# Gate logits of an expert choice taken from another layer's turned tokens, with both scales applied by VectorE

## The chip, the cores and the metric

One Trainium2 chip, one of its cores. The time is the device time of the whole kernel in microseconds (us); lower is better. The kernel before takes 2459.57 us (median of three runs).

## The reference, cut to what matters

Four images x of 56 x 56 tokens with 128 channels pass four layers. The change lies in the last one, on tokens t of shape (4, 3136, 128):

```python
t = t + attn(ln(t))        # scores exp(-|q-k|^2), softmax over them, times V = ln(t) @ Wv.T
t = t + choice(ln(t))

def choice(x):             # 64 experts choose tokens
    logits = einsum('bsd,ed->bse', x, gate_w) + gate_b
    probs = softmax(logits, axis=1)                 # over the tokens
    vals, idx = top_k(probs.transpose(0, 2, 1), 8)  # 8 tokens for each expert
    pooled = einsum('bked,bke->bed', x[idx], vals)
    out = mlp_of_each_expert(pooled)                # weight1, gelu, weight2
    return zeros.at[idx].add(out * vals)
```

ln takes the mean from each token and divides by the deviation. Where all scores of `attn` are far below what float32 tells from 0, its output is the same for each token: the mean of V. The kernel computes that mean, checks by bounds (`bounds`, `decide`) that the scores are so, and has a second program for inputs where they are not.

## The kernel before, in words

An image has NT = 28 tiles of P = 112 tokens, in NG = 7 groups of GT = 4 tiles (GW = 448 tokens). x lives in SBUF with tokens on partitions. A product over channels needs them turned: ScalarE normalises a group to `xn` (`normal`, L1693, four instructions), TensorE transposes it in four (`transposed`, L208) and ScalarE copies the result out of PSUM.

Stages: layer 0 for all images (to about 575 us), then the softmax attention of layer 2 for images 0 to 3 (`Attention.run`; s_ps L2066 the scores, e L2073 the exponentials, o_ps L2149 the products with the values; to about 2246 us), then a tail for image 3 and the experts. While the attention of image i runs, the other layers of earlier images run as *background*: each is a list of pieces with a cost (`costing`), lists are merged by their due places (`merged`), and `Paced` calls pieces between the attention's matmuls. `background(2)` holds the mixture and far attention of images 0 and 1 and the choice of image 0; `background(3)` the same for image 2 and the choice of images 1 and 2; `trail` starts image 3's. The order of each engine is settled when the program is built and does not move at run time. SP (SyncE) issues nearly all DMAs, in its order.

`FarAttention.image` makes, for each group, `xn`, `xnT` (with the sums for the mean), `products` (q_near, k_near) and `with_norms`; `mean` turns the sums into v (L1880 to L1887), and `add` adds v to every token (L1892; image 3: groups 3 and up on GpSimd). `ExpertChoice.steps` then needs, for the tokens x + v:

- `statistics`: L2301, four an image group on VectorE
- `root`: `moments` (L936 to L939), then 1/deviation by Newton steps on VectorE (`inverse_root`, L914 to L924), and the offset L2307
- `store`: x and rs to DRAM `rows`, 129 floats a token, for the gather
- `tokens`, `turned`, `logits`: normalised tokens (L1693, or L1688 on GpSimd), four transposes (L208), copy zT (L2322), matmul with gate_w (L2327), copy to `taken` (L2331), maximum of eight (L2332)
- `choose`: the top eight over the image (L2350), where they are (L2351), the gather of their rows; `marked`, `weighed`, `gather`, `pooled`: exponentials and the mean of the chosen tokens

Image 3's last mixture group, its mean, adds, statistics, roots, logits and choice stand in an order written out by hand (`manual_schedule` in `layers_of_safe_scores`), with `beside` putting bounds between them. There GpSimd makes some roots as a power (`span_norms`, L1673). `experts` then streams the weights of 64 experts, four at a time: 32 lots of 1 MB (L2263), nine ahead. Each step ends with a copy `found` out of PSUM (L2482) and four DMAs to `out0` and `out1` (L2489); `found` has two buffers. `scatter` spreads the outputs to the tokens (L2529, L2541).

PSUM banks of kind "one" (`flow.one`, four) serve all the small products.

Of the kernel before, what the change touches and what calls it, by code (L numbers as in the profile page):

```python
# [9 lines left out]
F32 = mybir.dt.float32  # L10
BF16 = mybir.dt.bfloat16
AF = mybir.ActivationFunctionType
ALU = mybir.AluOpType
# [4 lines left out]
B, H, W, C = 4, 56, 56, 128  # L18
# [1681 lines left out]
class FarAttention:  # L1700
# [13 lines left out]

    def __init__(self, env, ctx, flow, work):
        self.env, self.flow, self.work = env, flow, work
        nc, ins = env.nc, env.ins
        self.cp = cp = ctx.enter_context(env.tc.tile_pool(name="d_const", bufs=1, side="right"))  # L1720
        self.small = ctx.enter_context(env.tc.tile_pool(name="d_small", bufs=2, side="right"))

        self.even = ctx.enter_context(ExitStack())
        self.held = [
            stack.enter_context(env.tc.tile_pool(name=name, bufs=1, side="right"))
            for stack, name in ((ctx, "d_odd"), (self.even, "d_even"))
        ]


        norm = work.tile([128, GW], F32, tag="xnT_m", name="norm")[:, : 2 * 129]  # L1730
        norm = norm.rearrange("p (i c) -> p i c", i=2)
        nc.sync.dma_start(norm, ins["norm_channels"])
        self.norm = cp.tile([128, 2, 128], BF16, tag="norm16", name="norm16")
        nc.vector.tensor_copy(self.norm, norm[:, :, :128])
        self.one = cp.tile([128, 2, 1], F32, tag="one16", name="one16")
        nc.vector.tensor_copy(self.one, norm[:, :, 128:129])
        self.q_w = cp.tile([128, NR, 32], F32, tag="q_w", name="q_w")
        self.k_w = cp.tile([128, 32], F32, tag="k_w", name="k_w")
        nc.gpsimd.memset(self.q_w, 0.0)
        nc.gpsimd.memset(self.k_w, 0.0)  # L1740
        self.far = cp.tile([128, 1], F32, tag="far", name="far")
        self.half = cp.tile([128, 1], F32, tag="half", name="half")


        n = B * NG * (NR * NC + 1)
        self.found = cp.tile([128, n], F32, tag="found", name="found")
        nc.gpsimd.memset(self.found, 0.0)
        self.most, self.sums = 0, n

    def weights(self):  # L1750
# [23 lines left out]
            nc.vector.tensor_reduce(part[:, i : i + 1], square, AX.X, ALU.add)  # L1774

        def of_values():
            ps = flow.one([128, 512], "w_ps")
            nc.tensor.transpose(ps[:, :C], loaded("w_v", ins["L3_attn_Wv"]), env.ident)
            self.v_w = cp.tile([128, C], F32, tag="v_w", name="v_w")
            nc.vector.tensor_copy(self.v_w, ps[:, :C])  # L1780

        def bound():
            ps = flow.one([128, 512], "n_ps")
# [10 lines left out]
    def image(self, b, spans, places="d"):  # L1794
# [1 line left out]


        env, nc, flow, sp = self.env, self.env.nc, self.flow, self.small
        x = env.x[b]
        held = {"q": {}}  # L1800
        pool = self.held[1 - b % 2]

        def turned(g):
            if g == 0:
# [73 lines left out]
        def mean():  # L1878
            total = sp.tile([128, 1], F32, tag="x_total", name="x_total")
            nc.vector.tensor_reduce(total, held["sums"], AX.X, ALU.add)  # L1880
            nc.vector.tensor_scalar(total, total, 1.0 / TOK, None, ALU.mult)
            v_ps = flow.one([128, 512], "v_ps")
            nc.tensor.matmul(
                v_ps[:P, :C], total.to_broadcast([128, P]), self.v_w, start=True, stop=True
            )
            held["v"] = v = sp.tile([P, C], F32, tag="v", name="v", bufs=1)
            nc.vector.tensor_copy(v, v_ps[:P, :C])  # L1887

        def add(g):
            tiles = slice(g * GT, (g + 1) * GT)  # L1890
# [5 lines left out]

        def of(span):
            take, norm = span_norms(env, sp, b, span, places)

            def tokens(g):  # L1900
                held["xn"] = normal(
                    env, self.work, places, b, g, norm, span, places == "t" and g == NG - 1
                )

            return [costing(1.8 * len(span), take)] + sum([
                [
                    costing(0.6, lambda g=g: tokens(g)), costing(0.6, lambda g=g: turned(g), True),
                    costing(0.8, lambda g=g: products(g), True),
                    costing(1.2, lambda g=g: with_norms(g), True),
                ]  # L1910
                for g in span
            ], [])
# [305 lines left out]
class ExpertChoice:  # L2218
# [9 lines left out]
    def __init__(self, env, ctx, flow):  # L2228
# [7 lines left out]
        for half in range(2):  # L2236
# [14 lines left out]
        self.rows = [  # L2251
            dp.tile([TOK, C + 1], F32, tag=f"rows{b}", name=f"rows{b}") for b in range(B)
        ]
        self.fold = cp.tile([2 * EC, EC], F32, tag="fold", name="fold")
        nc.gpsimd.tensor_tensor(self.fold, env.ident[:, :EC], env.ident[:, EC:], ALU.add)
        self.lots, self.at = {}, 0

    def weights(self, pool, units):

# [2 lines left out]
            self.lots[u] = w = pool.tile([128, ET, HID], F32, tag="lot", name="lot")  # L2262
            self.env.nc.sync.dma_start(w, self.env.ins["L3_ffn_lots"][u // 2][:, u % 2])  # L2263

    def pieces(self, b, places="d"):

        steps = self.steps(b, places, [range(NG)])
        first = [costing(1.8, lambda g=g: steps["statistics"](g)) for g in range(NG)]
        first.append(costing(3.0, lambda: steps["root"](range(NG))))
        first.append(costing(0.1, lambda: steps["store"](range(NG))))  # L2270
        for g in range(NG):
            for cost, name, apart in (
                (0.5, "tokens", False), (0.5, "turned", True), (1.4, "logits", True)
            ):
                first.append(costing(cost, lambda name=name, g=g: steps[name](g), apart))
        return first + [
            costing(5.0, steps["choose"]), costing(5.0, steps["marked"]),
            *[costing(0.7, lambda g=g: steps["weighed"](g)) for g in range(NG)],
            costing(0.1, steps["gather"]), costing(1.0, steps["pooled"], True),
        ]  # L2280

    def steps(self, b, places, norms_of):
# [20 lines left out]
        def root(groups):  # L2303
            of = slice(groups[0] * GT, (groups[-1] + 1) * GT)
            mean2, var = moments(env, sp, f"c{len(groups)}", st[:, of, :])
            inverse_root(env, sp, var, rs[:, of])
            nc.vector.scalar_tensor_tensor(off[:, of], mean2, -0.5, rs[:, of], ALU.mult, ALU.mult)  # L2307
            if groups[0] == 0:
                held["best"] = sp.tile([2 * EC, NG * KT], F32, tag="best", name="best", bufs=1)

# [13 lines left out]
        def logits(g):  # L2324
# [6 lines left out]
            nc.scalar.copy(taken[:, cols], l_ps[rows, :GW])  # L2331
            nc.vector.max(held["best"][rows, g * KT : (g + 1) * KT], l_ps[rows, :GW])  # L2332

        def store(groups):
            of = slice(groups[0] * GT, (groups[-1] + 1) * GT)
            rows_of = self.rows[b].rearrange("(t p) c -> p t c", p=P)
            nc.sync.dma_start(rows_of[:, of, :C], x[:, of, :])
            nc.sync.dma_start(rows_of[:, of, C : C + 1], rs[:, of].unsqueeze(2))
# [52 lines left out]
        def pooled():  # L2391
# [10 lines left out]

        return dict(
            statistics=statistics, root=root, store=store, tokens=tokens, turned=turned,
            logits=logits, choose=choose, marked=marked, weighed=weighed, gather=gather,
            pooled=pooled,
        )

    def experts(self, ctx, pool, units, others=()):
# [3 lines left out]
        self.at = units  # L2413
        self.late = ctx.enter_context(env.tc.tile_pool(name="e_late", bufs=2))
        self.outs = [
            self.late.tile([2 * EC, C], F32, tag=f"out{i}", name=f"out{i}", bufs=1) for i in range(2)
        ]
        self.more = pool
        for out in self.outs:
# [52 lines left out]
        def second(q):  # L2472
            o_ps = flow.ps_sums.tile([128, 512], F32, tag="o", name="o_ps")
            for c in range(HC):
                for i in range(ET):
# [2 lines left out]
                        self.lots[2 * q + 1][:, i, c * C : (c + 1) * C],  # L2478
                        start=(c == 0), stop=(c == HC - 1), skip_group_check=True,
                    )  # L2480
            found = self.late.tile([128, C], F32, tag="found", name="found")
            nc.vector.tensor_copy(found, o_ps[:, :C])  # L2482
            if q == NQ - 1:
                self.found = found
# [21 lines left out]
    def scatter(self):  # L2506

        env, nc, flow = self.env, self.env.nc, self.flow
        for pair in range(2):
# [1 line left out]
            o_ps = flow.ps_sums.tile([128, 512], F32, tag="o", name="o_ps")  # L2511
            nc.tensor.matmul(o_ps[:, :C], self.pick[:, pair, :], self.found, start=True, stop=True)
            nc.vector.tensor_tensor(out, out, o_ps[:, :C], ALU.add)
            bias = self.late.tile([2 * EC, C], F32, tag="c_bias", name="c_bias")
            nc.vector.tensor_scalar(bias, self.bias2, self.inverse[pair], None, ALU.mult)
            nc.vector.scalar_tensor_tensor(
                out, out, self.inverse[pair], bias, ALU.mult, ALU.add
# [379 lines left out]
def layers_of_safe_scores(env: Env, f, soft):  # L2897
    with ExitStack() as ctx:
# [61 lines left out]
            )  # L2960

        def chosen(b):
            return listed("far", held["choice"].pieces(b))

        def to_mixture():
            right.close()
            flow.to_pieces()
            held["choice"] = ExpertChoice(env, right, flow)
            held["far"] = far = FarAttention(env, right, flow, held["choice"].work)
            held["mixture"] = Mixture(env, mixing, flow, held["choice"].work)  # L2970
            run_all(far.weights())

# [33 lines left out]
        with tc.manual_schedule(  # L3006
# [2 lines left out]
                mybir.EngineType.Pool,  # L3009
            }  # L3010
        ):
            *tail, products, with_norms = held["tails"][-1]
            beside("scalar", 5)
            run_all(tail[:6])
            run_all(tail[6:10])
# [9 lines left out]
            def each(name, groups):  # L3025
                run_all([lambda g=g: of[name](g) for g in groups])

            for g in late:
                add[g]()
            for g in early:  # L3030
                add[g]()
# [1 line left out]
                beside("scalar", 1)  # L3033
            of["root"](early)
            of["store"](early)
            each("statistics", late)
            beside("scalar", 1)
            of["tokens"](0), of["tokens"](1), of["turned"](0), of["logits"](0)
            of["root"](late)
            of["store"](late)  # L3040
            of["turned"](1), of["tokens"](2), of["logits"](1), of["turned"](2), of["logits"](2)
            beside("scalar", 1)
            of["tokens"](3), of["tokens"](4), of["turned"](3)
            of["tokens"](5), of["logits"](3), of["turned"](4)
            of["tokens"](6), of["logits"](4), of["turned"](5), of["logits"](5)
            of["turned"](6), of["logits"](6)
            of["choose"]()
            beside("scalar", 2)
            products()
# [87 lines left out]
```

## Time and profile before

| | us |
|---|---|
| runs | 2459.57 (median), 2459.46, 2461.65 |
| profiled execution: its time | 2462.98 |
| its span | 2461.18 |
| PE busy in the span | 2337.9 (95%) |
| DVE busy | 1816.2 (74%) |
| ACT busy | 1550.7 (63%) |
| POOL busy | 293.8 (12%) |
| mean granted clock of TensorE | 0.965 |

PE is TensorE's matmuls and PEld its weight loads, DVE VectorE, ACT ScalarE, POOL GpSimd. A group's line names line, engine, operation, output<-inputs and shapes, its count, busy us and mean ns of one, and after the second bar the idle time of the engine just before it and what ended it. In the views by slices a digit is the busy share in tenths; PEclk is the clock granted to TensorE, in tenths of full speed. The chain is followed back from the last instruction, at each step to what released it.

### The profile page before, as it was taken

Reading aid. Unit: us, or ns where it says so; the run is one execution under the profiler, and the core shown is the slowest. Engines: PE = TensorE matmul, PEld = TensorE weight load, DVE = VectorE, ACT = ScalarE, POOL = GpSimd, SP = SyncE. Lnnn points to the kernel's source line nnn. Section 1 sums busy time; section 2 is a strip of 40 time slices with the busy share of each in tenths; the row PEclk is TensorE's granted clock in tenths of the full one; section 3 lists DMA queues with packets and bytes.
Section 4 is the critical chain, followed back from the end, with each engine's and each line's share of the span. In section 5 each row is a group of like instructions: output and inputs, shape, how many; then the busy total and the mean of one; then the engine's idle time right before and its main releaser. Section 6 shows DMA issues by size and latency. Waiting matters only on the chain.

```text
span 2461.2 us, 38767 instructions
## 1 busy us (share of the span) xinstructions
PE 2337.9 (95%) x14357; PEld 1258.2 (51%) x14357; DVE 1816.2 (74%) x4816; ACT 1550.7 (63%) x3346; POOL 293.8 (12%) x578
## 2 busy tenths in 40 slices
PE   6999999999999999999999999999999998998585
PEld 4777777775455555555554444445444443433134
DVE  5666899983997958799678777854788576776554
ACT  4999889875666646676332556575545566775553
POOL 4423363320000000000000000100000001011302
PEclk9999999999999999999999999999999997998578
DMA  5100000000000000000000010000000010100676
GB/s 124 36 8 2 2 2 2 2 2 9 1 1 1 1 1 0 1 1 1 12 1 0 1 27 1 5 1 1 1 1 1 1 27 5 27 5 1 184 297 206
DMA packets 65642, 61.42 MB, mean 25 GB/s; under 512 B 17048, under 2 KB 60915, under 8 KB 61348
## 3 DMA queue, kind: packets, MB, share of 16 engines
q1 hardware_dynamic: 64932, 57.80, 8.4%
q8 instruction: 115, 1.88, 0.3%
q0 software_dynamic: 512, 1.06, 0.2%
q14 instruction: 83, 0.68, 0.1%
HBM read 45.83 MB, written 12.90 MB: 24 GB/s over the span
## 4 chain that ended last, share of the span: by engine, by line
PE 63%; DVE 6%; ACT 2%; DMA 2%; issue 2%; POOL 1%; SPq 0%; DVEq 0%; POOLq 0%; ACTq 0%
PE s_ps L2066 20%; PE o_ps L2149 20%; PE y_ps L1574 7%; PE d_ps L1861 3%; PE xT_ps L208 2%; PE g_ps L1207 2%; DMA lot<-in_L_ffn_lots 2%; PE l_ps L2327 1%; PE y_ps L2090 1%; PE z_ps L2042 1%; PE q_ps L1825 1%; DVE found L1867 1%; PE l_ps L1534 1%; ACT xn L1693 1%; DVE gated L1587 1%
## 5 line engine op out<-in xcount | busy, mean ns | idle before, releaser
L2073 ACT ACTIVATE e<-s_ps 128x448 f32<-128x448 f32 x688 | 366.5, 541 | 491.8 <-PE s_ps L2066 486.1
L2066 PE MATMUL s_ps<-zT,xnT 128*128 128x448 f32 (+1 forms) x1400 | 649.4, 554 | 0.0
L2149 PE MATMUL o_ps<-e,keep 128*128 128x448 f32 (+1 forms) x1376 | 648.5, 554 | 0.0
L2149 PEld LDWEIGHTS o_ps<-e,keep 128*128 128x128 f32 (+1 forms) x1376 | 241.7, 190 | 217.8 <-issue 217.2
L2066 PEld LDWEIGHTS s_ps<-zT,xnT 128*128 128x128 f32 (+1 forms) x1400 | 241.1, 189 | 213.9 <-issue 193.5
L1873 ACT ACTIVATE d_ps<-d_ps,half 128x448 f32<-128x448 f32 (+1 forms) x376 | 227.2, 605 | 88.0 <-PE d_ps L1861 86.3
L1867 DVE TENSOR_REDUCE found<-d_ps 128x1 f32<-128x448 f32 x324 | 196.9, 619 | 77.6 <-PE d_ps L1861 75.7
L1574 PE MATMUL y_ps<-experts,xnT 128*112 128x512 f32 x448 | 217.0, 608 | 0.0
L1587 DVE TENSOR_TENSOR gated<-y_ps,gate 112x512 f32<-112x512 f32 x220 | 148.8, 686 | 35.5 <-PE y_ps L1574 33.0
L1593 DVE TENSOR_TENSOR gated<-gated 112x512 f32<-112x512 f32 x330 | 151.8, 467 | 3.5
L1861 PE MATMUL d_ps<-q_near,k_near 32*128 32x448 bf16 (+1 forms) x700 | 135.4, 374 | 15.6 <-ACT d_ps L1873 10.0
L208 PE MATMUL xT_ps<-ident,xn 112*128 112x112 f32 x672 | 117.8, 283 | 34.1 <-ACT xn L1693 26.0
L208 PEld LDWEIGHTS xT_ps<-ident,xn 112*128 112x128 f32 x672 | 80.4, 147 | 113.5 <-ACT xn L1693 58.9
L1673 POOL TENSOR_TENSOR g_rs<-var,exponent 112x4 f32<-112x4 f32 x17 | 17.9, 1053 | 1006.3 <-DVE var L1672 895.3
L1574 PEld LDWEIGHTS y_ps<-experts,xnT 128*112 128x112 f32 x448 | 77.2, 180 | 98.9 <-issue 63.8
L1861 PEld LDWEIGHTS <-k_near 32*128 32x128 bf16 (+1 forms) x700 | 32.0, 92 | 181.2 <-issue 167.2
L1693 ACT ACTIVATE xn<-x,g_off,g_rs 112x128 f32<-112x128 f32 x220 | 93.2, 486 | 26.3 <-DVE g_off L1675 13.0
L677 DVE TENSOR_TENSOR e<-e,band 112x1792 f32<-112x1792 f32 (+3 forms) x56 | 99.9, 1788 | 10.2 <-ACT e L670 10.2
L782 PE MATMUL f_ps<-w_fc,h 128*112 128x128 f32 x896 | 104.8, 274 | 1.9 <-ACT h L773 1.6
L782 PEld LDWEIGHTS f_ps<-w_fc,h 128*112 128x112 f32 x896 | 99.8, 177 | 5.2 <-ACT h L773 4.8
L768 PE MATMUL h_ps<-zT,w_fc 128*128 128x448 f32 x224 | 88.9, 540 | 0.6 <-ACT zT L762 0.6
L670 ACT ACTIVATE e<-s_ps 112x1792 f32<-112x1792 f32 (+3 forms) x56 | 82.6, 1476 | 6.3 <-PE s_ps L661 3.3
(427 smaller groups left out, 3939.7 us busy)
## 6 DMA issues: line engine op xcount, KB each, us to landing
lot<-in_L_ffn_lots SPq DMA_DIRECT2D x32, 1024.0 KB
out_x<-x SPq DMA_DIRECT2D x28, 224.0 KB
x<-in_x SPq DMA_DIRECT2D x3, 1568.0 KB
rows<-x SPq DMA_DIRECT2D x3, 1568.0 KB
x<-in_x SPq DMA_DIRECT2D x7, 224.0 KB
parts<-in_waves SPq DMA_DIRECT2D x8, 173.0 KB
out<-found SPq DMA_DIRECT2D x60, 2.0 KB
rows<-x SPq DMA_DIRECT2D x1, 896.0 KB
```

The lines of the kernel that those rows point to most:

```text
L208: self.nc.tensor.transpose(ps[:, j * P : (j + 1) * P], xn[:, j, :], self.ident[:P, :P])
L782: nc.tensor.matmul(f_ps[:, j, :], h[:, k, j * P : (j + 1) * P], w_fc2[:, k, :], start=(k == 0), stop=(k == 3),)
L1574: nc.tensor.matmul(y_ps, held["xnT"][g][:, j * P : (j + 1) * P], self.experts[:, 4 * i : 4 * i + 4, :], start=True, stop=True,)
L1587: nc.vector.tensor_tensor(gated[:, some, :], y_ps, gate[:, some].unsqueeze(2).to_broadcast([P, 4, C]), ALU.mult,)
L1593: by.tensor_tensor(gated[:, :n, :], gated[:, :n, :], gated[:, n : 2 * n, :], ALU.add)
L1693: env.nc.scalar.activation(xn[:, j, :], env.x[b][:, g * GT + j, :], AF.Identity, bias=norm["off"][:, i : i + 1], scale=norm["rs"][:, i : i ...
L1861: nc.tensor.matmul(d, held["k"][part, 128 * c : 128 * c + n], held["q"][g][part, :], start=True, stop=True,)
L1867: nc.vector.tensor_reduce(self.found[:, self.most : self.most + 1], d, AX.X, ALU.max)
L1873: nc.scalar.activation(d, d, AF.Relu, bias=self.half[:n], accum_out=self.found[:n, self.sums : self.sums + 1],)
L2066: nc.tensor.matmul(s_ps[i * n : (i + 1) * n, :GW], self.xnT[:, at : at + n], zT, start=True, stop=True,)
L2073: nc.scalar.activation(e[:n], s_ps[:n, :GW], AF.Exp)
L2149: nc.tensor.matmul(sums[:, :GW], self.keep[:n, k, :], e[:n], start=(k == 0 and g - 1 not in pairs), stop=last,)
```

## The change

The logits of token t are gate_w (centred over its channels) times (x + v), times 1/deviation of x + v. The change takes gate_w x from the far attention's `xnT`, which is already turned: x minus its mean, over x's deviation. VectorE multiplies by that deviation (`logits` in `FarAttention.image`), so the raw products lie in `taken` before v is known. When v is there, `mean` makes the column `moved` = gate_w v, and `moved(g)` adds it and multiplies by the new 1/deviation.

Both scales belong to tokens, which here lie along the free axis, on 64 partitions. For images 0 to 2 they are stored to DRAM (`keep_scales`, four bytes a token) and fetched back as rows over 64 partitions (`fetch_scale`); the choice's rows are asked for ahead, in the order fetch 0, fetch 1, moved 0, fetch 2, moved 1 and so on. For image 3's choice, and its last group in the far attention, TensorE spreads them (`spread`, four matmuls a group). Image 3's roots become a power on GpSimd, and the early one stands between GpSimd's additions. To make room, `out0`, `out1` and `c_bias` take places of other tiles, and `found` has one buffer.

```diff
 class FarAttention:
         def of_values():
+            self.choice.centre()
...
+            nc.tensor.matmul(
+                ps[:, C : C + EC], w_v, self.choice.gate_w, start=True, stop=True
+            )
...
         def mean():
...
+            m_ps = flow.one([128, 512], "m_ps")
+            nc.tensor.matmul(m_ps[rows, :1], self.v_w[:, C:], total, start=True, stop=True)
+            nc.scalar.copy(choice.moved[b // 2][rows], m_ps[rows, :1])
...
+            def deviations():
+                held["sd"] = sd = sp.tile([P, n], F32, tag=f"g_sd{n}_{places}", name="g_sd", bufs=1)
+                nc.vector.reciprocal(sd, norm["rs"])
+                if not final:
+                    choice.keep_scales(b, 0, span, sd)
...
             def tokens(g):
...
+                held["row"] = row = sp.tile([128, GW], F32, tag=f"row_{places}", name="row", bufs=1)
+                if not final:
+                    choice.fetch_scale(row[rows], b, 0, g)
+
+            def logits(g):
+                cols, row = slice(g * GW, (g + 1) * GW), held["row"][rows]
+                if final:
+                    ps = flow.one([128, 512], "sd_ps")
+                    choice.spread(ps, rows, held["sd"])
+                    nc.scalar.copy(row, ps[rows, :GW])
+                l_ps = flow.one([128, 512], "l_ps")[rows, :GW]
+                nc.tensor.matmul(l_ps, choice.gate_w, held["xnT"], start=True, stop=True)
+                nc.vector.tensor_tensor(raw[:, cols], l_ps, row, ALU.mult)
 class ExpertChoice:
+    def keep_scales(self, b, i, span, scale):
+        self.env.nc.sync.dma_start(
+            self.scales[b][i].rearrange("g (j p) -> p (g j)", p=P)[
+                :, span[0] * GT : (span[-1] + 1) * GT
+            ].unsqueeze(2),
+            scale.unsqueeze(2),
+        )
+    def fetch_scale(self, row, b, i, g):
+        self.env.nc.sync.dma_start(row, self.scales[b][i][g].partition_broadcast(EC))
+    def spread(self, ps, rows, scale):
+        for j in range(GT):
+            self.env.nc.tensor.matmul(
+                ps[rows, j * P : (j + 1) * P], scale[:, j : j + 1].to_broadcast([P, EC]),
+                self.env.ident[:P, :P], start=True, stop=True,
+            )
...
+        for g in range(NG + 1 if from_raw else 0):
+            if g < NG:
+                first.append(costing(0.1, lambda g=g: steps["fetched"](g)))
+            if g:
+                first.append(costing(1.4, lambda g=g: steps["moved"](g - 1)))
...
         def root(groups):
...
+            if last:
+                nc.vector.tensor_scalar(var, var, 1e-5, None, ALU.add)
+                nc.gpsimd.tensor_tensor(
+                    rs[:, of], var, env.exponent[:P, : var.shape[1]], ALU.pow
+                )
...
+        def moved(g):
+            cols = slice(g * GW, (g + 1) * GW)
+            part = taken[:, cols]
+            if last:
+                ps = flow.one([128, 512], "rs_ps")
+                self.spread(ps, rows, rs[:, g * GT : (g + 1) * GT])
+                nc.vector.scalar_tensor_tensor(
+                    part, part, self.moved[b // 2][rows], ps[rows, :GW], ALU.add, ALU.mult
+                )
+            else:
+                nc.vector.scalar_tensor_tensor(
+                    part, part, self.moved[b // 2][rows], held.pop(("scale", g)),
+                    ALU.add, ALU.mult,
+                )
+            nc.vector.max(held["best"][rows, g * KT : (g + 1) * KT], part)
+
         def store(groups):
             of = slice(groups[0] * GT, (groups[-1] + 1) * GT)
+            if not last:
+                self.keep_scales(b, 1, groups, rs[:, of])
...
-            found = self.late.tile([128, C], F32, tag="found", name="found")
+            found = self.late.tile([128, C], F32, tag="found", name="found", bufs=1)
...
 layers_of_safe_scores, image 3:
-            for g in late:
+            for g in late[:2]:
                 add[g]()
...
             of["store"](early)
+            for g in late[2:]:
+                add[g]()
             each("statistics", late)
-            beside("scalar", 1)
-            of["tokens"](0), of["tokens"](1), of["turned"](0), of["logits"](0)
+            logits()
+            beside("scalar", 2)
+            each("moved", early)
             of["root"](late)
             of["store"](late)
...
+            each("moved", late)
             of["choose"]()
```

## The prediction

> **What bounds the kernel now.** I read the page's slices first, then its chain of work that ended last.
>
> ```profile
> PE   6999999999999999999999999999999998998585
> DVE  5666899983997958799678777854788576776554
> ACT  4999889875666646676332556575545566775553
> PEclk9999999999999999999999999999999997998578
> ...
> PE 63%; DVE 6%; ACT 2%; DMA 2%; issue 2%; POOL 1%; SPq 0%; DVEq 0%; POOLq 0%; ACTq 0%
> ```
>
> TensorE is busy in every slice up to about 2246 us and VectorE and ScalarE are not; 63% of the chain is TensorE's. So until image 3's attention ends, work taken from TensorE is worth its own time, and work added to VectorE or ScalarE costs only where TensorE then waits. From 2246 us on, in the tail, the clock falls and the chain changes hands: there each step is on the path. The change touches both.
>
> Next the groups of the removed lines, by line and shape (busy, mean ns of one, idle before):
>
> ```profile
> L1693 ACT ACTIVATE xn<-x,c_off,c_rs 112x128 f32<-112x128 f32 x98 | 42.2, 488 | 4.2 <-DVE c_off L2307 4.2
> L2322 ACT COPY zT<-xT_ps 128x448 f32<-128x448 f32 x28 | 14.9, 531 | 7.7 <-PE xT_ps L208 7.6
> L2331 ACT COPY taken<-l_ps 64x448 f32<-64x448 f32 x28 | 14.7, 526 | 20.5 <-PE l_ps L2327 20.5
> L2332 DVE MAX8 best<-l_ps 64x8 f32<-64x448 f32 x28 | 17.6, 628 | 27.6 <-ACT taken L2331 27.3
> L2377 DVE SCALAR_TENSOR_TENSOR taken<-marks,taken 64x448 f32<-64x448 bf16 x28 | 16.7, 615 | 0.3
> ```
>
> ScalarE loses 42.2 + 14.9 + 14.7 = 72 us over the kernel; the count of logits matmuls stays (28 groups, now fed by xnT). VectorE gets 28 products (0.65 each, by the 64-partition rows) and 28 additions-with-scale (0.62, as L2377).
>
> **Part 1: transposes, images 0 to 2.** 3 x 28 = 84 transposes leave the stretch that TensorE bounds. The timeline of TensorE gives the price: four start at 2034.44, and the next matmul starts at 2034.83, so 0.39 us for four, 0.0975 each. 84 x 0.0975 = **-8.2 us**. The four new m_ps and two w_ps matmuls are some tenths and are left out. If attention could not use the room, the gain would be nothing.
>
> **Part 2: the stretch at 2039 us.** In the windows of TensorE's clock one place of the main loop is not at full speed. The windows of tile s_ps, the attention scores, show what it costs (columns: us, PE, PEld, ACT busy, clock, DMA share, GB/s):
>
> ```profile
> 1900.00:1932.00 32.00, 9.42 (x23) 3.37 (x22) 5.42 (x10) 1.00 0.00 1
> 2039.00:2071.00 32.00, 2.24 (x3) 0.80 (x4) 1.51 (x3) 0.63 0.00 1
> 2071.00:2103.00 32.00, 11.49 (x26) 3.95 (x24) 6.39 (x12) 0.95 0.04 8
> ```
>
> o_ps (the products with the values) has 22, 0 and 20 records in the same three. So from 2039 to 2071 attention stands nearly still: 45 records usual, 3 done. There the choice of image 1 (transposes and logits, waiting on ScalarE's xn and zT) meets a boundary between two groups of image 3's attention, and TensorE's order, fixed at build time, has a long run without attention. Pairs of s_ps and o_ps start 0.75 us apart in full flow, 0.376 a record: 42 x 0.376 = 15.8 us lost. In the listing of the changed program the longest run of TensorE work with no attention matmul in it falls from about 10.1 us to 3.8 us (summed by such spacings). Some 2.7 us of this are the stretch's own transposes, counted above, so I take **-13 us**. Bounds: -4 (three quarters of it come back elsewhere, since the background work is still done) to -19 (the six slow microseconds after it go too).
>
> The Trainium skill ("TensorE: Matmul & The Clock Gate", section "What's actually happening") says the clock falls to half after an idle window of about 3.4 us and returns after a busy one. The row shows 0.63 in a stretch where TensorE counts 26.0 of 32 us busy: an average busy share hides such gaps. By the rule the whole loss would follow from one gap of 3.4 us, and any new wait that long would cost the same again.
>
> **Part 3: new waits for rows that pass through DRAM.** For images 0 to 2 VectorE now waits, at the first `moved`, until rs has been stored four bytes at a time in token order and one row has come back. The trace has such a store, the column rows<-c_rs, issued at 1475.17. The DMA view of 1474 to 1484:
>
> ```profile
> DMA  0000000057767997200000000020000000000000
> ...
> DMA packets 3153, 0.02 MB, mean 2 GB/s; under 512 B 3152, under 2 KB 3152, under 8 KB 3152
> ```
>
> Its packets end about 1478.5: 3.3 us after issue. A second store of this kind goes out right behind it, and the fetch needs an issue and a landing (1.55 us for the expert outputs when the DMA is idle, plus the wait for the store's end). So 6.5 to 7.8 us, middle 7.0. In the changed order VectorE has other work between the root's last operation and the first `moved`: about 4.4, 6.5 and 5.1 us for images 0, 1 and 2 (listing, by the rows' durations). What stays is 2.6 + 0.5 + 1.9 = 5 us of VectorE standing. Behind the waiting instruction stand L1867 reductions, `gated` products and xnT's statistics; TensorE waits for their PSUM banks (four of kind "one"), ScalarE for g_off. Part of the 5 us reaches TensorE: **+3 us**, from 0 (the banks cover it) to +10 (twice the wait, as two stores share the rings). The later rows are asked for two groups ahead (2.2 us of work against about 2.5) and add little; far's rows have at least 5 us and are hidden. SP gets some 60 more issues at about 0.5 us over 1,650 us; the 4-byte stores stand in its order just ahead of the 1.5 MB x store, whose only early reader is the gather, far later.
>
> VectorE's extra 21 x (0.65 + 0.62) = 26.7 us lie beside TensorE: none counted. ScalarE's relief (0.75 of 72 us, 54) is likewise counted at nothing: 0 to -8, since at 1500 to 1550 us it was busy 36 of 50.
>
> The skill's "DMA: Bandwidth & Descriptors" (sections "Anatomy of one DMA — SWDGE (gpsimd) path" and "Specifications") speaks against this change: about 2.0 us fixed per DMA, and writes under 512 bytes done by read-modify-write. By that figure alone a store and a fetch would be an estimated 4 us, less than the trace's own 3.3 us for the first store and what must follow it. The trace's is used.
>
> **Part 4: the tail, from v to the top scores.** The chain of waits ends the stretch like this:
>
> ```profile
> 2319.48 1.77 PE l_ps L2327 x2
> 2321.25 0.02 issue
> 2321.27 0.54 ACT taken L2331
> 2321.81 0.02 issue
> 2321.83 0.65 DVE best L2332
> 2322.48 0.02 issue
> 2322.50 0.23 DVE top L2350
> ```
>
> From v (2285.34) to `top` (2322.50) it is 37.2 us, mostly seven times transposes, zT and logits at half clock. After the change, from 2285.34: two adds on GpSimd (6.36 us for four, 1.59 each) to 2288.6; VectorE's adds, statistics and variance of the early groups, as now, but with L938 at its usual 0.18 instead of the 1.12 it took beside GpSimd, to 2291.3. The power runs on GpSimd; its nearest row is
>
> ```profile
> L1673 POOL TENSOR_TENSOR g_rs<-var,exponent 112x4 f32<-112x4 f32 x17 | 17.9, 1053 | 1006.3 <-DVE var L1672 895.3
> ```
>
> 112x12 lies between 1.05 (all fixed) and 3.15 (all per element); I take the middle, 2.1: 2293.4. Adds 5 and 6 behind it, 3.2: 2296.6. Last statistics 0.9: 2297.5. VectorE then has far's last product (0.65) and three early groups (0.62 + 0.64 each): 2302.0. Late variance 1.0, power 112x16 (1.05 to 4.2, taken 2.6): 2305.6. Spreading by four half-clock matmuls 1.1 and four last groups at 1.26, with 0.3 of semaphores: **2312.1, so -10.4 us**. Bounds -13 (powers at their fixed price) to -7.5 (at their full one). The experts' stream starts with the first lots' use, so it moves with it; the gather needs the rows' store, which landed at about 2315.8 and is asked for no earlier: little slack, inside the bounds.
>
> **Part 5: one buffer for `found`.** Each copy out of PSUM now waits for the landing of the previous pair's four stores (issued 0.54 apart, landing 1.55 after issue idle, 4 to 5 us after under the lots). Until 2417 the lots bound the loop. The last three copies come 3.65, 2.71 and 2.60 us after the one before; with one buffer a cycle is 0.32 + 3 x 0.54 + 1.55 = 3.5 or more, say 3.6: +2.0. The first outputs, and lots issued behind waiting stores: +1.5. **+3.5**, from +1 to +8 (every cycle loses half a microsecond).
>
> **Sum.** -8.2 - 13 + 3 - 10.4 + 3.5 = -25.1. Against the profiled execution, 2462.98 (span 2461.18), that is 2437.9; that execution stands 3.4 above the median of the runs, so 2459.57 - 25.1 = 2434.5, **2435 us**. All low ends together: -8.2 - 19 - 8 - 13 + 1 = -47.2, 2412; all high ends: 0 - 4 + 10 - 7.5 + 8 = +6.5, 2466.
>
> **Rivals.**
> *The stretch re-forms.* The same conflict of background work and attention arises at another place, as the order is made anew. For: image 1's choice still meets that boundary. Against: the listing's 3.8 us. Without -13 the sum is -12.1: 2447.
> *It takes the place of itself.* VectorE's waits at their high end and one buffer at +8: -8.2 - 4 + 10 - 10.4 + 8 = -4.6, 2455: no difference that a run can tell (within 0.2%, 4.9 us).
> *Slower: standing at the first `moved` starves TensorE.* VectorE holds four PSUM banks while it waits; when TensorE runs dry, the clock drops as at 2039 and each image loses what that place lost, 15.8 us. Three times 47 and the gains -8.2 - 13 - 10.4 + 3.5 = -28.1 make +19: 2479. It decides from a wait of about 4 us per image (the longest wait of TensorE's weight loads for xn between 1400 and 2245 was 3.8). For: no row in the trace has this round trip; against: 4.4 to 6.5 us of work ahead of it.
> *It does more.* ScalarE's relief shortens its own waits: 2415 to 2425.
>
> **How the numbers follow.** Forecast with its own spread of 2425 to 2443: 0.52. More: 0.16. Re-formed, 2443 to 2454: 0.15. No difference (2454.7 to 2464.5): 0.07. Slower: 0.10. The range must leave out at most 2 in 10: 2415 to 2457 leaves out the slower case, most of "no difference" and a little below. Faster by over 0.2%: 0.52 + 0.16 + 0.15 = 0.83.
>
> **What would show it.** Right: no place at 0.6 clock near 2040, with s_ps at over 20 records per 32 us there; 84 fewer transposes and the end of attention some 18 us earlier; `top` 27 us behind v; `found` copies at the end 3.6 us apart. Wrong: VectorE's idle time before `moved` above 4 us each, with weight loads waiting for banks; a new stretch of halved clock; powers of 4 us; lots issued late behind the outputs.

## The result, and the profile after

The changed kernel takes 2498.53 us (median of four runs, 2494.34 to 2501.39) against 2460.61 for the kernel before beside it: a ratio of 1.0152, 95% interval 1.0134 to 1.017. Slower by 38 us, where 25 us less were forecast. The profiled execution took 2496.7 us, its span is 2494.9.

From the page of the changed kernel, the slices and the head of the chain:

```profile
PE   6999999999999999999999997999999997988486
DVE  5666899974997959799598686844788676776644
ACT  4998888865666646666323444475545564645363
PEclk9999999999999999999999998999999998998687
DMA  5100000000000000000000013000000013410585
...
PE 50%; issue 13%; DVE 6%; DMA 4%; ACT 2%; POOL 2%; SPq 1%; DVEq 0%; POOLq 0%; ACTq 0%
```

The DMA row of the kernel before:

```profile
DMA  5100000000000000000000010000000010100676
```

ScalarE is less busy from the middle on, as it should be; but TensorE's row and its clock now dip in the slice of 1497 to 1559 us. The DMA row shows 1 and 3 around there, where it showed 1 and 0 before, and later 1, 3, 4, 1 for 1, 0, 1, 0. These six slices move only 18 to 36 GB/s, and over the span the packets rose from 65,642 to 91,180 with 67.0 MB for 61.4: many packets, few bytes. TensorE's share of the chain fell from 63% to 50%.

Times of the same events, read off the timelines (us; e is the exponential of the attention, 172 to an image; the last column is the experiment with turned stores, below):

| | before | after | turned stores |
|---|---|---|---|
| first e of image 2 | 1229.3 | 1228.0 | 1227.9 |
| from there to the first e of image 3 | 473.9 | 496.3 | 477.3 |
| from there to the last e | 539.0 | 555.3 | 523.5 |
| last e to v | 42.9 | 44.5 | 43.9 |
| v to `top` | 37.4 | 28.0 | 27.8 |
| `top` to the end | 138.7 | 142.9 | 142.6 |

Nearly all of the loss lies in the main loop: +22.4 and +16.3. The tail gained 9.4 from v to `top` (1.6 were lost ahead of v), the experts lost 4.2.

General windows of the changed kernel (us, then PE, PEld, DVE, ACT, POOL busy, clock, DMA share, GB/s) show three stretches of one kind:

```profile
1500.00:1525.00 25.00, 13.59 (x39) 5.58 (x39) 12.30 (x25) 8.54 (x24) 0.00 (x0) 0.73 0.48 28
2050.00:2075.00 25.00, 15.80 (x59) 5.95 (x58) 11.99 (x44) 10.49 (x30) 1.01 (x1) 0.91 0.82 15
2175.00:2200.00 25.00, 15.19 (x38) 5.46 (x37) 14.27 (x34) 6.11 (x16) 0.00 (x0) 0.80 0.80 31
```

VectorE and TensorE are idle for 37% to 52% of these stretches, and the DMA engines are busy with 15 to 31 GB/s. VectorE's and TensorE's waits from 1360 to 2290 us say on what (us in total, how many, the longest):

```profile
DVE taken L2430 <- DMA scale<-scale: 35.1, 5, 12.0
...
PE d_ps L1869 <- DVE gated L1587: 15.2, 5, 11.4
PE xT_ps L208 <- ACT xn L1693: 12.8, 4, 11.9
PE y_ps L1574 <- DVE gated L1587: 9.8, 1, 9.8
```

VectorE stands 12.0, 11.4 and 10.5 us at the first `moved` of the three images, and TensorE stands behind it, for a PSUM bank (`gated` not read yet) or for xn (g_off not made yet): the longest waits of TensorE's three lines, 11.4, 11.9 and 9.8, pair off with the three stands. The first stand in the timelines of SP and VectorE (in brackets, the idle time before the instruction):

```profile
1493.87 0.31 SPq L2306 DMA_DIRECT2D scale<-c_rs  x1
1494.22 1.86 SPq L2442 DMA_DIRECT2D rows<-c_rs  x1
1505.65 19.77 SPq L2315 DMA_DIRECT2D scale<-scale  x7
```

```profile
1510.08 0.68 DVE L2430 SCALAR_TENSOR_TENSOR taken<-taken,moved,scale 64x448 f32<-64x448 f32 x1 [12.02 <-DMA scale<-scale]
```

SP does not issue the first fetch until 11.8 us after the store: it has to wait for the landing, that is until the stored data may be read. The row takes another 4.4. The prediction had 6.5 to 7.8 us for all of it. The packets of this pair of stores fill the DMA engines nearly as long, to about 1505 (DMA view of 1493 to 1513, half a microsecond a digit):

```profile
DMA  0003779999999999999999998300011261200032
```

The far attention's store alone is late too, with nothing behind it:

```profile
1629.24 0.31 SPq L2306 DMA_DIRECT2D scale<-g_sd  x1
1639.20 0.44 SPq L2315 DMA_DIRECT2D row<-scale  x1
```

10.0 us, though its packets are over 4.0 us after the issue. Here the packets end long before the reader may go. Image 3's stores of only 448 elements take 6.2 to 7.0 us to the next issue, their packets 1.3.

### The profile page after: what moved, and what is told of

The parts are those of the page before. It is cut to its first block, busy times and chain, and to the rows that moved or that the text cites. A ratio compares the mean times of both kernels' runs of the same rounds, so it can differ in the third digit from the quotient of the medians.

```text
span 2494.9 us, 38673 instructions
## 1 busy us (share of the span) xinstructions
PE 2339.8 (94%) x14321; PEld 1261.9 (51%) x14321; DVE 1836.8 (74%) x4859; ACT 1490.0 (60%) x3197; POOL 291.5 (12%) x566
## 2 busy tenths in 40 slices
DMA packets 91180, 67.04 MB, mean 27 GB/s; under 512 B 39512, under 2 KB 86451, under 8 KB 86884
## 3 DMA queue, kind: packets, MB, share of 16 engines
q1 hardware_dynamic: 90468, 63.40, 11.3%
## 4 chain that ended last, share of the span: by engine, by line
PE 50%; issue 13%; DVE 6%; DMA 4%; ACT 2%; POOL 2%; SPq 1%; DVEq 0%; POOLq 0%; ACTq 0%
PE o_ps L2180 16%; PE s_ps L2097 16%; PE y_ps L1574 4%; PE d_ps L1869 3%; PE g_ps L1207 2%; PE xT_ps L208 1%; DMA out<-found 1%; DMA scale<-g_sd 1%; DVE found L1875 1%; DVE gated L1587 1%; PE z_ps L2073 1%; PE y_ps L2121 1%; ACT d_ps L1881 1%; PE l_ps L1932 1%; PE y_ps L2634 1%
## 5 line engine op out<-in xcount | busy, mean ns | idle before, releaser
L2180 PE MATMUL o_ps<-e,keep 128*128 128x448 f32 (+1 forms) x1376 | 655.4, 559 | 0.0
L1875 DVE TENSOR_REDUCE found<-d_ps 128x1 f32<-128x448 f32 x324 | 196.1, 617 | 48.8 <-PE d_ps L1869 46.7
L208 PE MATMUL xT_ps<-ident,xn 112*128 112x112 f32 x560 | 92.6, 278 | 32.8 <-ACT xn L1693 24.8
L208 PEld LDWEIGHTS xT_ps<-ident,xn 112*128 112x128 f32 x560 | 64.7, 145 | 86.2 <-ACT xn L1693 46.9
```

The costliest lines, as they stand in the source:

```text
L208: self.nc.tensor.transpose(ps[:, j * P : (j + 1) * P], xn[:, j, :], self.ident[:P, :P])
L1875: nc.vector.tensor_reduce(self.found[:, self.most : self.most + 1], d, AX.X, ALU.max)
L2180: nc.tensor.matmul(sums[:, :GW], self.keep[:n, k, :], e[:n], start=(k == 0 and g - 1 not in pairs), stop=last,)
```

## The experiments

The theory after this look (landing): the loss is VectorE's stand for scales whose small stores land late. Rivals: the order of the engines, made anew, is worse by itself (A); small packets slow what runs beside them (B; the traces speak against it: between a small store and its fetch VectorE's reductions L1875 take 0.616 us and ScalarE's exponentials 0.543, both medians, and elsewhere in the loop the same); the way through DRAM costs this whatever the packets (C).

**Old scales.**

```diff
-            self.fetch_scale(scale, b, 1, g)
+            self.fetch_scale(scale, b, 0, g)
```

> The choice's rows come from the deviations that the far attention stored some 60 to 100 us earlier; all stores and fetches stay, and every instruction keeps its place, but VectorE no longer waits for a store that was just issued. Left out: the right new scale (the logits of images 0 to 2 carry a wrong factor). Landing theory (VectorE stands 12.0, 11.4 and 10.5 us at the first `moved` of the three images, and TensorE behind it): the stands go and the time falls by 30 to 40 us from 2498, to 2458 to 2468. Rival A (the order made anew, without the transposes, is worse for TensorE by itself): no change, 2493 to 2500. Rival B (the 4-byte packets themselves slow everything beside them): no change either, as they stay.

Measured: 2485.41 us, 13 less than the changed kernel, as much as two builds of it differ (below). Neither theory's number. The order did not stay, against the expectation: with its data ready, the first fetches and `moved` came ahead of the root. At image 0 the stand at `moved` is gone, but another stands in its place, for the gather of rows whose column was stored just before:

```profile
DVE c_mean L2498 <- POOL c_got L2493: 10.7, 1, 10.7
```

At images 1 and 2 fetches that wait for nothing were issued 2 to 3 us behind the two small stores, and VectorE still stood 10.2 and 10.4 us for them. So whatever comes behind small stores waits, by a semaphore or in the queue; A is not shown, and the test was not clean.

**Turned stores.**

```diff
 def keep_scales(self, b, i, span, scale, turned):
+        nc, n = self.env.nc, len(span) * GT
+        ps = self.flow.one([128, 512], "s_ps")
+        nc.tensor.transpose(ps[:n, :P], scale, self.env.ident[:P, :P])
+        nc.scalar.copy(turned[:n, :P], ps[:n, :P])
-            self.scales[b][i].rearrange("g (j p) -> p (g j)", p=P)[
+            self.scales[b][i].rearrange("g (j p) -> (g j) p", p=P)[
...
-            scale.unsqueeze(2),
+            turned[:n, :P],
```

> TensorE turns the scales (112 x 28 to 28 x 112, one transpose and one ScalarE copy) ahead of each store, so that a store is 28 rows of 448 bytes in place of 3136 elements of four bytes, for the far attention and the choice alike. Nothing is left out. Landing theory with small packets as the cause: a store lands within 3 us in place of 10 to 12, the stand at the first `moved` falls from 11 to 0 to 3 us each, far's rows come in time, time 2452 to 2466. Rival C (the way through DRAM costs this much whatever the packets): stands of 8 us and more, 2485 or above. Rival A (order): no change.

Measured: 2444.80 us, ratio to before 0.9933 (0.9916 to 0.9950). That is 7 below the landing theory's band and at least 40 below what C and A had; both fall: the way through DRAM, the `moved` pieces and, but for image 0, the new order are all still there. A store of 3136 values now lets the fetch go 1.4 us after its issue (4.2 and 5.0 for the choice of images 1 and 2, where the column of `rows` goes out just ahead):

```profile
1950.72 0.31 SPq L2311 DMA_DIRECT2D scale<-turned  x1
1952.09 0.45 SPq L2320 DMA_DIRECT2D row<-scale  x1
```

VectorE's waits for scales sum to 5.0 us in place of 35.1. (For image 0 the transpose also stands 22 us later in TensorE's order, and other work fills the time; so there the shorter landing is not the only help.)

**Only the choice's stores turned** (the far attention keeps the old ones).

```diff
 def store(groups):
-                self.keep_scales(b, 1, groups, rs[:, of])
+                self.keep_turned(b, 1, groups, rs[:, of], turned)
```

> Only the choice's stores are turned; the far attention keeps its four-byte stores side by side. Nothing is left out. Landing theory: the stands at the first `moved` go (34 us in the trace of the changed kernel, and what the clock loses with them), the far rows' waits stay (about 9 us of VectorE, and SP held for 6 to 11 us each time): 2452 to 2464. If the far attention's stores were the larger part of the loss: 2475 or above.

Measured: 2457.51 us. This splits the loss. From the first e of image 2 to the last e the changed kernel takes 1051.6 us, this one 1013.5, all stores turned 1000.8: the choice's small stores cost 38.1 us, the far attention's 12.7, 50.8 together. (Two other kernels below have the changed kernel's main loop and take 1061.0 and 1066.9 us there, so the sum can as well be 9 to 15 more.) The far ones act through the rows (waits of 19.1 us in seven, the longest 4.5).

**Elements apart.** The scales 64 bytes apart in DRAM:

```diff
-            [dp.tile([NG, GW], F32, tag=f"scale{i}{b}", name=f"scale{i}{b}") for i in range(2)]
+            [dp.tile([NG, GW, 16], F32, tag=f"scale{i}{b}", name=f"scale{i}{b}") for i in range(2)]
```

> The scales' elements lie 64 bytes apart in DRAM, in place of side by side; the store has the same 3136 elements of four bytes, and the fetch still reads 448 floats side by side (so image 0 to 2 get wrong scales, which is left out; the places between are filled once, ahead of the loop). If the landing is late because of the count of small elements, SP issues the first fetch 10 to 12 us after the store as now. Rival F (neighbouring four-byte writes hold each other up): the first fetch goes out 4 to 5 us after the store, and VectorE's stands fall to 2 to 5 us.

Measured: 2475.19 us in one run. From the timeline of SP, a store of 448 and one of 3136 elements, each with the fetch behind it:

```profile
1868.45 0.31 SPq L2312 DMA_DIRECT2D scale<-g_sd  x1
1870.17 0.44 SPq L2321 DMA_DIRECT2D row<-scale  x1
```

```profile
1960.28 0.31 SPq L2312 DMA_DIRECT2D scale<-g_sd  x1
1965.94 0.45 SPq L2321 DMA_DIRECT2D row<-scale  x1
```

1.7 us in place of 6.4, and 5.7 in place of 10 to 11.4, with as many packets. So rival F is right for some 5 us of each landing: four-byte writes side by side land later than the same writes apart. The rest of a 3136-element store, some 4 us over a turned one or over 448 elements, goes with the count. VectorE's waits fell to 24.2 us, the longest 8.8, not to 2 to 5: the pair of stores still needs 6 to 7 us, and the row comes after.

**Column of `rows` late.** The second small store moved behind the last `moved`:

```diff
 def choose():
+            if not last:
+                nc.sync.dma_start(
+                    self.rows[b].rearrange("(t p) c -> p t c", p=P)[:, :, C : C + 1], rs.unsqueeze(2)
+                )
             nc.vector.max(top, held["best"][rows])
```

> The second four-byte store of the choice (1/deviation into `rows`, for the gather) is issued after the last `moved` in place of right behind the first; nothing is left out. Landing theory: one store alone still lands 10 to 11 us after issue (as the far attention's does in the trace of the changed kernel), the stands at the first `moved` shrink by 1 to 3 us each: 2490 to 2497. Rival E (two stores on the same rings are the cause, one alone lands with its packets at about 4 us): stands of 4 us, 2472 to 2480.

Measured: 2511.79 us; but the edit did nothing. The store needs only the root, and in the built program it stands where it stood, 0.35 us behind the first. VectorE's and SP's orders there are those of the changed kernel. So this is a second build of the same thing, 13 us slower: its small stores took 0.2 to 1.8 us longer each. It says how much a time that hangs on such landings can move; why they are longer here is open. Rival E falls by the far attention's stores: alone, with no second one behind, they land after 10.0 to 11.4 us in the changed kernel, against 11.8 to 12.1 for the pairs.

**Column behind the turned store.** In a version with turned stores and two places for `found`, the column is written from the turned tile and issued behind the scales:

```diff
 def store(groups):
                 self.keep_scales(b, 1, groups, rs[:, of], turned)
+                nc.sync.dma_start(
+                    self.rows[b].rearrange("(t p) c -> t p c", p=P)[:, :, C : C + 1],
+                    turned[:NT, :P].unsqueeze(2),
+                )
```

> As the kernel before it in this list, but the four-byte column of `rows` is written from the turned scales and issued right behind the choice's scale store, where it went out ahead of it (by 0.7 to 22 us). Nothing is left out. With the turned store SP still issued the first fetch of images 1 and 2 some 4 to 5 us after the store, against 1.4 for image 0, where the column had gone out long before. Theory (the column's 3136 small elements hold up the store behind them): 1.2 to 2 us from store to first fetch for all three images, time 0 to 5 us lower, 2437 to 2443. Rival (the fetch then queues behind the column instead): the wait moves to the fetch, same time.

Measured: 2454.05 us, worse by 11 than the same version without it (2443.09). The first half of the theory holds: the fetch goes out 1.3 to 1.4 us after the store at all three images. Then the rival takes over: the fetches queue behind the column, VectorE waits 12.3 us for them in place of 6.9, and the seven issues of an image spread over 16 to 29 us (11 to 23 without).

**The tail alone.** Images 0 to 2 the old way, so image 3's tokens, tail and `found` are the change (the choice's scale store stayed in, read by nobody):

```diff
-            return listed("far", held["choice"].pieces(b, from_raw=True))
+            return listed("far", held["choice"].pieces(b))
...
 def of(span):
+            if not trailing:
...
```

> Images 0 to 2 go the old way (transposes, zT, logits); only image 3 takes the logits from the far attention's turned tokens, with the roots on GpSimd and one `found`. Landing theory: the main loop ends where it ended before (2242 us in the trace), give or take the row waits of image 3's own groups (0 to +4), the tail gains 9.5 and the experts lose 4: 2454 to 2460. Rival A (the tail's own part of the change is to blame for the loss in the main loop, by way of the order): 2475 or above.

Measured: 2475.38 us, above the band, at the figure that rival A was given. The main loop ends 13.2 us later than before, the tail and the experts are as expected (27.7 and 143.5 us). The next one asks why.

**The tail alone, no scale through DRAM.** All rows of image 3 by `spread`, no store:

```diff
 def logits(g):
+                if by_pe:
+                    nc.scalar.copy(raw[:, cols], l_ps)
+                    nc.vector.tensor_tensor(raw[:, cols], raw[:, cols], ps[rows, :GW], ALU.mult)
...
 def store(groups):
-                self.keep_scales(b, 1, groups, rs[:, of])
```

> As the tail-only kernel, but image 3's far attention gets all its rows by TensorE's spreading, and the choice of images 0 to 2 stores no scale: no scale passes through DRAM at all. Landing theory: the 13 us that the tail-only kernel lost in the main loop were the waits for image 3's rows; the loop ends at 2240 to 2245 in the trace, the tail gains 9.5, the experts lose 4: 2453 to 2459. Rival A (the new order): 2465 or above.

Measured: 2467.54 us. The loop still ends 9.8 us late. TensorE's work from 1870 us to the last e, before and here:

```profile
1870.00:2242.00 372.00, 361.30 (x1232) 146.01 (x1230) 268.15 (x774) 240.42 (x621) 25.45 (x34) 0.96 0.07 11
```

```profile
1870.00:2252.00 382.00, 372.29 (x1285) 151.48 (x1284) 273.05 (x791) 244.68 (x630) 25.23 (x35) 0.96 0.07 11
```

53 records and 11 us more of TensorE, up to the same event. Image 3's logits were in the tail before; now five of its seven groups have them while TensorE bounds the loop: two records at 0.376 each, 0.75 a group, 3.8 us. A spread matmul, unlike a transpose, leaves two records also (sd_ps has 56 for 28 matmuls): eight a group, some 0.8 us, 3.9 more. By this estimate 7.7 of the 9.8 are work, and at most 2 are left for the order (A). In the changed kernel itself, with five of image 3's rows through DRAM, only the 3.8 apply.

**Two places for `found`.**

```diff
+            if q % 2:
                 found = self.late.tile([128, C], F32, tag="found", name="found", bufs=1)
+            else:
+                found = self.work.tile([128, GW], F32, tag="xnT_t", name="found", bufs=1)[:, :C]
```

> `found` in the expert loop has two places again (the second is a tile that is free by then). One-buffer theory (the loop waits for the landing of the previous outputs): the stretch from the top scores to the end falls from 142.9 to about 139 us, time lower by 3 to 5 us. Rival D (the 1 MB lots bound the loop anyway): within 1 us of the changed kernel.

Measured: 2503.79 us, 5 above the changed kernel. The stretch in question did as the theory said: `top` to the end 139.5 us in place of 142.9. The rest is the main loop, in the same order on every engine, with landings again longer (12.3 to 12.8 in place of 11.8 to 12.1 for the pairs): 10 us later at its end.

**All mended, and the best version.** Turned stores, image 3's rows by `spread` (as just shown), the late column (which again went out early, ahead of the store) and two places for `found`; then turned stores and two places for `found` alone. No new lines.

> The full change with its waits mended: scales turned by TensorE ahead of the store, image 3's rows by spreading, the `rows` column stored after the last `moved`, two places for `found`. Nothing is left out. Landing theory with the one-buffer term: 2444.8 less 3.4 for `found`, less 1 to 5 for rows and order: 2436 to 2441. Rival (found is hidden by the lots, rows were covered already): 2443 to 2446.

Measured: 2449.18 us, ratio 0.9949 (0.9932 to 0.9967): above the band, and from turned stores alone the runs do not tell it apart. Its image 3 takes 528.5 us to the last e, against 523.5. That the spreading's records cost more than the rows' waits did, now that the stores land early, would fit, but is not shown. The last one leaves the spreading out:

> The turned store together with two places for `found`; nothing is left out. The main loop and the tail as with the turned store (2444.8), the stretch from the top scores to the end 2 to 3.5 us shorter: 2441 to 2443. Rival D (the lots bound the expert loop): 2444 to 2446.

Measured: 2443.09 us (2439.89 to 2449.86), ratio to before 0.9928 (0.9914 to 0.9942): faster than both kernels, by 0.7% than the one before. `top` to the end is 141.1 in its profile, 1.5 less than with turned stores alone. From the turned stores alone (2444.80) the runs do not tell it apart.

## Why the prediction was wrong, point by point

**What bounds the kernel** was right: TensorE until the last e, and the stages after it as read.

**Transposes (-8.2) and the stretch at 2039 (-13)** were right in kind. (The records of o_ps stand in the prediction in another order than its windows: there are 20, 0 and 22, so usual are 43 to 48 in all, and 15 to 17 us were lost.) With turned stores, the windows of s_ps at the former gap:

```profile
2008.00:2040.00 32.00, 12.01 (x26) 4.00 (x26) 6.76 (x14) 1.00 0.37 56
2040.00:2072.00 32.00, 11.51 (x24) 4.12 (x24) 5.95 (x11) 1.00 0.12 34
```

No gap, full clock. But what the main loop gained there is 12.1 us (1012.9 to 1000.8), not 21.2. A term of the other sign was missed: "the count of logits matmuls stays" holds for the kernel, not for the bound stretch. Of 28 logits 21 lay there before and 26 after, at 0.75 each: +3.8. Of the other five, the waits that are left (5.0 us of VectorE for scales) may be a part; they were not taken apart.

The clock rule that the prediction sets beside the row of 0.63 does not come out of it: TensorE's longest idle time there is 2.7 us, and it begins at 2046.9, when by the trace's clock records TensorE had been at half since 2045.9 (to 2069.8). In the changed kernel, where TensorE stands 11.4, 11.9 and 9.8 us, the clock is at half for 13.7, 13.7 and 10.2 us, 3 to 7 of them past the stand. So a long wait cost mostly itself: by the experiment with the choice's stores 12.7 us each, for 11.3 of standing.

**The waits for rows (+3, from 0 to +10)** is the step that failed: in place of 3 us the main loop lost 50.8 (the changed kernel against turned stores). It took the end of one store's packets ("Its packets end about 1478.5: 3.3 us after issue") for the landing. No row of the trace before shows a landing: the gathers that read that column come 44 to 86 us after it for images 0 to 2 and 21 us after for image 3, and none waits for it, so 3.3 was a lower end only, and the reader of the trace had no upper one. The row was not quite the same case either: the values of the column lie 516 bytes apart in DRAM, the scales side by side, and against 64 bytes apart that cost some 5 us of a landing. Measured, a store side by side releases its reader after 10 to 12 us, and with the row it is 16.0 to 16.3 us (1493.87 to 1510.08 for image 0) against 4.1 to 6.0 us of other work ahead, close to the 4.4 to 6.5 foreseen. Two more parts of the step were wrong. The PSUM banks cover almost nothing: of VectorE's 33.9 us TensorE stands 33.1. And far's rows, "hidden" there, cost 12.7. What stands behind the waiting instruction, and who waits for it, was said rightly.

The page "DMA: Bandwidth & Descriptors" of the Trainium skill (section "Specifications") has transfers below 512 bytes as read-modify-write. By it rows of 448 bytes and single values of four bytes are alike, while the runs tell them apart: 1.4 us and 10 us for the same data. No run shows the read-modify-write itself. The prediction's estimate of 4 us rests on a fixed cost of about 2.0 us, which the page (section "Anatomy of one DMA — SWDGE (gpsimd) path") gives for DMAs issued by GpSimd, while SP issues these; it and the trace's 3.3 us, which was used instead, were both far too low.

**The tail (-10.4)** was right in its sum: -9.4. Powers were 2.28 and 2.91 us (taken 2.1 and 2.6); in the chain of the changed kernel

```profile
2341.36 2.92 POOL c_rs L2380
2344.32 6.25 PE rs_ps L2320 x32
2350.59 0.70 DVE taken L2426
2351.32 0.64 DVE best L2434
2351.97 0.23 DVE top L2454
```

the spreading is longer than thought: 6.25 us for four groups, 1.56 each, at half clock by its two records a matmul, not 1.1 once. It runs on beside the additions and maxima of the earlier groups, which the prediction had put one after the other, so the two misses nearly cancel (from the second power's end to `top` 7.7 us, where 6.4 was said), which is luck.

**One `found` (+3.5)** was right: +4.2 here, and 3.4 back with two (1.5 between the two kernels with turned stores). The last three copies come 3.60, 3.70 and 3.61 us after the one before, where 3.6 was said.

**The rivals.** The slower one named the mechanism, its place and its threshold of 4 us; its 47 us are close to the 50.8, but in part by luck: it priced three stands at 15.8 us by the clock, while the stands cost 38.1 in all, mostly by their length, and the rest came from far's stores, which it does not name. 2479 fell short since the gains were overstated. It got 0.10 because 4.4 to 6.5 us of cover were held against a round trip that had no measured end.

## What to carry to other kernels

The end of a DMA's packets in a trace is not the time when its reader may go (4.0 against 10.0 us here): price a new round trip through DRAM only by a store of the same layout that somebody in the trace waits for, and where there is none, keep a wide upper end. Turn a per-partition column before storing it in token order; one transpose and one copy ahead of each store were worth 54 us here. And when work is moved between stages, count it by stage: what is unchanged in total can have moved under the engine that bounds.

## What the runs showed of the hardware

Issue of a store to issue of the fetch that waits for it, on SP's queue:

| store | 448 values | 3136 values | 3136, `rows` column right behind |
|---|---|---|---|
| 4 bytes each, side by side (changed kernel) | 6.2 to 7.0 us | 10.0 to 11.4 | 11.8 to 12.1 |
| 4 bytes each, 64 bytes apart (one run) | 1.7 to 3.7 | 5.5 to 5.8 | 6.0 to 7.1 |
| rows of 448 bytes (all kernels that have them) | 1.1 to 2.0 | 1.3 to 1.4 | 1.3 to 1.4 |

In the other kernels with stores side by side the first row goes up to 8.8, 13.2 and 12.8 us, and once to 14.3 for 448 values, behind a 1.5 MB store. With the column right ahead of a turned store the fetch went out 4 to 5.5 us after it. Two builds with the same order of instructions differed by 13 us (2498.53 and 2511.79; the kernel before took 2460.61 and 2461.98 beside them) where such landings were on the path; what made them differ was not tested.
